# Three edits of order in a two-layer graph network: the first two groups, the seam between the passes, and the last group

## The chip, the cores and the metric

The kernel runs on one core of a Trainium2 chip. The metric is the device time of one execution in microseconds (us). The core has five engines, each with its own instruction queue that is worked off in order: PE (TensorE: matrix products; PEld is its weight load), DVE (VectorE), ACT (ScalarE), POOL (GpSimd) and SP (SyncE, here the issuer of nearly all DMAs). Every engine waits on semaphores for what the others produce. An instruction that waits holds up all that stand behind it on its engine.

## The reference

64 batches of 256 nodes with 512 features go through two layers. Everything is float32.

```python
# layer 0
h = relu(layernorm(x))                                    # per row of 512
x = x + einsum('bnd,do->bno', einsum('nm,bmd->bnd', adj, h), weight) + bias
# layer 1: 8 heads of 64
h = relu(layernorm(x))
q, k, v = h @ Wq + bq, h @ Wk + bk, h @ Wv + bv
scores = einsum('bqhd,bkhd->bhqk', q, k) / sqrt(64) + (1 - adj) * -1e9
x = x + einsum('bhqk,bkhd->bqhd', softmax(scores), v) @ Wo + bo
```

## The kernel before

**Groups and passes.** Two batches make a group, so there are NG = 32 groups, numbered 0 to 31. The first pass runs layer 0 over all groups and leaves two things in DRAM for each: the new x (`residual_g`) and its normalised, rectified and turned form (`hidden_g`). The second pass runs layer 1 over all groups. Between the two lies a seam: the last group of the first pass and the first group of the second.

**Products with seven instead of eight parts.** Every product of a weight with a group is cut into 2x2 blocks and done with seven block products (Strassen's scheme in Winograd's form). Its sums of operand blocks are prepared ahead. For activations they are named t1 to t4: t1 = b12 - b11, t2 = b22 - t1, t3 = b22 - b12, t4 = b21 - t2 (L442 to 446, class `Halves`). t2 needs t1, t4 needs t2, t3 needs neither. Written in capitals, T2 and T3 are the same two. For weights the sums are s1 to s4. In `project` (L456) the seven products follow one another on PE: a11·b11, a12·b21, s2·t2, s3·t3, s1·t1, a22·t4, s4·b22. The chain a11, s2·t2, s1·t1, s4 accumulates in one PSUM bank ("a"), and s3·t3, a22·t4 in another ("c"). Between two accumulations, another engine reads the bank out: where a product follows in the same bank, PE waits for this reading. In the second pass, from group 2 on, three of the seven are cut once more (`project2`, L541), and `block_sums_of` (L891) makes their inner sums (`both.sums` from the tokens, `last.sums` from t4) on POOL.

**Layer 0 of one group.** `moments` (L40) and `norm_scales` (L46, four small instructions on POOL named rs and nb) give the scales, `relu` in `ready` (L691) makes h on ACT. `feature_sums` (L745) and `last_feature_sum` make s1, s2, s3 and s4 of h on POOL, tile hs; s3 overwrites a part of h. `adjacency` (L759) multiplies h by the transposed adjacency matrix in seven products named py_ga, py_gb, py_gc; its own t1 to t4 of the adjacency matrix are made once by `adjacency_sums` (L734, tile adjT_t, four instructions on POOL). The result yT gets its t1 to t4 (tile t_y) on POOL. `layer0` (L810) multiplies by the weight (banks w_ga, w_gb, w_gc, of which a and c are filled with the bias by `seeded` on ACT, L255), adds x, takes the second moments, and leaves residual and hidden. Group 0 has a path of its own, `first_adjacency` (L710), with plain products py.

**Attention of one group and half.** `queries_keys` and `values` run seven products each for q, k and v. `score` (L964) multiplies q and k of one half of the heads (qd = 0 or 1), in four pieces numbered by c and b; DVE scales and masks (L980), POOL subtracts the row `top` (L986; in the last group piece c + b = 2 goes to DVE, L984), ACT takes exp (L991), POOL adds up two halves of keys (`key_sum`, L998, tile as). `attend` (L1000) multiplies by ones (pden, the denominators) and by v (pav), DVE inverts and multiplies (oT, L1027 and L1045), then the sums of oT (tile t_o) follow for the output product in `post`.

**What sets the order.** Nothing is scheduled automatically. The program is one list written out by hand with a clock: `tick()` advances it, `after(n, f)` puts f n ticks later, and what is due at one tick is put down in the order in which it was entered. The generators (`project`, `adjacency`, `layer0`) give control back after each product, and `run` ticks after each. So a number in `after` decides behind which instructions of its engine a piece of work stands; it sets no time. In pass 1 the loop at L1103 takes one product of `layer0(g)` and n products of `adjacency(g + 1)` per tick, with n from a list of seven. `ready`, `hidden_sums`, `score` and `attend` take such delays as arguments.

**The end.** `stats` collects sums that show an overflow; DVE reduces them to one number (L1165, L1166), PE multiplies it by ones (pf, L1168), DVE turns it into an integer (`flag`), and all engines read the flag to decide on a slower path that is not taken here.

Of the kernel before, what the change touches and what calls it, by code (L numbers as in the profile page):

```python
# [198 lines left out]
def kernel(  # L199
# [16 lines left out]
    nc = tc.nc  # L216
# [7 lines left out]
    NG = B // GB  # L224
# [42 lines left out]
    def after(delay, fn, *args):  # L267
        entered[0] += 1
        later.append((clock[0] + delay, entered[0], fn, args))
# [584 lines left out]
    H1T, HH, HO = {}, {}, {}  # L854
# [106 lines left out]

    A, AS = {}, {}

    def score(g, qd, sum_delay):  # L964


        pair = [act.tile([P, GB, 2 * NT, N], F32, tag="h", name=f"a_{g}_{qd}_{c}", bufs=2) for c in range(2)]
        for c in range(2):
            for b in range(GB):
                ps = [bank([P, NT * N], f"sc_{g}_{qd}_{c}{b}_{j}") for j in range(2)]  # L970
                q, k = Q[g][qd, b], K[g][qd, b]
                for kt in range(NT):
                    for j in range(2):
                        nc.tensor.matmul(ps[j][:, kt * N:(kt + 1) * N],  # L974
                                         k[j * HD:(j + 1) * HD, c, kt * P:(kt + 1) * P],
                                         q[j * HD:(j + 1) * HD, c, :], start=(kt == 0), stop=True,
                                         skip_group_check=True)
                a = A[c, b] = pair[c][:, b]
                for j in range(2):
                    nc.vector.scalar_tensor_tensor(a[:, j * NT:(j + 1) * NT, :].rearrange("p k n -> p (k n)"),  # L980
                                                   ps[j], SCALE, maskT_f, op0=ALU.mult, op1=ALU.add)
                    give(ps[j])
                if g == NG - 1 and c + b == 2:
                    after(2, lambda a: nc.vector.tensor_tensor(a, a, top_b, op=ALU.subtract), a)  # L984
                else:
                    nc.gpsimd.tensor_tensor(a, a, top_b, op=ALU.subtract)  # L986
                after((3, 4, 5, 8 if sum_delay > 3 else 6)[2 * c + b], exponent, a)
                after(sum_delay + 2 * c + b, key_sum, g, qd, c, b)

    def exponent(a):  # L990
# [9 lines left out]
    def attend(g, qd):  # L1000


        pd = bank([P, GN], f"pden_{g}_{qd}")
        po = [bank([P, GN], f"pav_{g}_{qd}_{f}") for f in range(2)]
        for b in range(GB):
            for h in range(4):
                nc.tensor.matmul(pd[h * 32:(h + 1) * 32, b * N:(b + 1) * N], ones[:, 0:32], AS[h // 2, b][:, h % 2, :],  # L1007
                                 start=(b == 0), stop=True, tile_position=(0, h * 32), skip_group_check=True)
        for b in range(GB):
            v = V[g][qd, b]  # L1010
            for k in range(NT):
                for f in range(2):
                    for h in range(4):
                        nc.tensor.matmul(po[f][h * 32:(h + 1) * 32, b * N:(b + 1) * N],  # L1014
                                         v[:, k, h * HD + f * 32:h * HD + f * 32 + 32],
                                         A[h // 2, b][:, (h % 2) * NT + k, :],
                                         start=(b + k == 0), stop=(k == NT - 1), tile_position=(0, h * 32),
                                         skip_group_check=True)
        i = g * HQ + qd
        if i == 0:  # L1020
            AS["rest"] = act.tile([P, 4, GN], F32, tag="yT1", name="rest")
        den, rden = AS["rest"][:, 0, :], AS["rest"][:, 1, :]
        nc.scalar.activation(den, pd, AF.Identity, accum_out=stats[:, 0, i:i + 1])  # L1023
        give(pd)

        def invert(c):
            nc.vector.reciprocal(rden[:, c * P:(c + 1) * P], den[:, c * P:(c + 1) * P])  # L1027

        early = 2 if g >= FIRST2 and (g, qd) != (NG - 1, 1) else 4
        for c in range(early):  # L1030
            invert(c)
        if qd == 0:

            last = g == NG - 1
            OT[g] = (xpool if last else act).tile([P, DC, GN], F32, tag="x" if last else "r", name=f"oT_{g}")
            HO[g] = Halves(f"o_{g}", [OT[g][:, :, k * N:(k + 1) * N] for k in range(GB)], 0 if last else 1)

        def note():
            nc.scalar.activation(den, rden, AF.Identity, accum_out=stats[:, 1, i:i + 1])

        def divide():
            for c in range(early, 4):
                invert(c)
            for f in range(2):
                nc.vector.tensor_tensor(OT[g][:, 2 * qd + f, :], po[f], rden, op=ALU.mult)  # L1045
                give(po[f])
            after(2 if (g, qd) == (NG - 1, 1) else 3, note)
            wait = 7 if (g, qd) == (NG - 2, 1) else 0
            sums = lambda: HO[g].sums(nc.gpsimd, ("t3", "t2", "t4") if qd else ("t1",))
            if wait:  # L1050
                after(wait, sums)
            else:
                sums()
            if qd and g >= FIRST2:
                block_outputs(g, nc.gpsimd, wait + 1 if g >= NG - 2 else 2)

        after(1, divide)

    def run(gen, steps=99):

        for _ in zip(range(steps), gen):
            tick()
# [12 lines left out]

    ready(0, (0, 0, 2, 2), (0, 2), (1, 1, 3, 3), batches=2)
    load(1)
    ready(1, (4, 4, 4, 4), (4,), (5, 5, 6, 6))
    after(6, feature_sums, 1)
    after(7, last_feature_sum, 1)  # L1080
    tick()
    turn_adjacency()
    adjacency_sums()
    split_bias(b0_r)
    tick()
    weight_sums(nc.vector, w0_sb, "0", (0, 0, 6, 7))
# [3 lines left out]
    steps = first_adjacency()  # L1090
# [3 lines left out]
    for g in range(NG - 1):  # L1094
        for fn, *args in side[g]:
            fn(*args)

        if g + 2 < NG:
            ready(g + 2, (1, 1, 1, 1), (1,), (3, 3, 3, 3))
            after(4, feature_sums, g + 2)  # L1100
            after(5, last_feature_sum, g + 2)
        weighted, turned = layer0(g, seeds), adjacency(g + 1)
        for i, n in enumerate((0, 0, 0, 1, 1, 2, 3) if g == 0 else (1, 1, 2, 2, 1, 0, 0)):  # L1103
            next(weighted)
            for _ in range(n):
                next(turned)
            if i == 5:
                seeds = seeded(b0_r, f"w_{g + 1}")
            tick()
            if i == 2 and g + 3 < NG:  # L1110
                load(g + 3)
        for rest in (weighted, turned):
            for _ in rest:
                pass
        if g == NG - 3:
            load_hidden(0)
    load_hidden(1)
    hidden_sums(0, 1, 1, 2, 2)
    steps = layer0(NG - 1, seeds)
    run(steps, 4)  # L1120
    run(queries_keys(0))
    score(0, 0, 6)
    tick()
    run(steps)
    hidden_sums(1, 1, 2, 6, 7)
    run(values(0))
    for g in range(NG):
        attend(g, 0)
        load_residual(g)
        if g + 2 < NG:  # L1130
            load_hidden(g + 2)
        score(g, 1, 5 if g < NG - 1 else 3)
        tick()
        if g == 0:
            for n, tag in ((4 * DC, "w0_sb"), (4, "w0_s1"), (4, "w0_s2"), (4, "w0_s4"), (4, "adjT"), (4, "b0_r")):
                t = const.tile([P, n, P], F32, tag=tag, name=f"spare_{tag}")
                spare.extend(t[:, i, :] for i in range(n))
        for n, at in (("q", 7),) if g == 0 else (("k", 1), ("v", 5)) if g == 1 else (("o", 2),) if g == 2 else ():
            for i, work in enumerate(block_sums(n)):
                after(at + i // 3, *work)  # L1140
        if g + 1 < NG:
            run(queries_keys(g + 1))
        else:
            last = post(g - 1, seed_outputs(g - 1))
            run(last, 6)
        attend(g, 1)
        if g + 1 < NG:
            score(g + 1, 0, 5)
            tick()
            steps = values(g + 1)  # L1150
            run(steps, 5)
            seeds = seed_outputs(g) if g + 2 < NG else None
            run(steps)
            if g + 2 < NG:
                hidden_sums(g + 2, 2, 3, 4, 5)
                if g + 2 >= FIRST2:
                    block_hidden(g + 2, 6)
                run(post(g, seeds))
# [5 lines left out]
    worst = small.tile([P, 1], F32, tag="worst", name="worst", bufs=1)  # L1164
    nc.vector.tensor_scalar(bad, stats.rearrange("p s i -> p (s i)"), BOUND, None, op0=ALU.is_gt)  # L1165
    nc.vector.tensor_reduce(worst, bad, AX.X, ALU.max)  # L1166
    pf = bank([1, 1], "pf")
    nc.tensor.matmul(pf, worst, ones[:, 0:1], start=True, stop=True)  # L1168
    nc.vector.tensor_copy(flag, pf)
# [36 lines left out]
```

## Time and profile before

| | us |
|---|---|
| three runs | 2666.66, 2666.79, 2671.13 |
| median | 2666.79 |
| the profiled execution | 2666.74 |
| its span (first to last instruction) | 2664.9 |

Busy time in that span: PE 2626.7 us (99%), POOL 1989.0 (75%), DVE 1865.7 (70%), ACT 971.8 (36%). PE is idle for 38.2 us in all: 9.4 before its first instruction, 7.0 after its last product, and the rest in gaps of 0.3 to 4.7 us in three places, the first 57 us, the seam (612 to 664 us) and the last 57 us. From 70 to 612 us, and from 670 to 2608 us, PE is busy in every slice.

In the timeline a row is: start, duration from the first to the last instruction of the row, engine, line, operation, tile written <- tiles read, shapes, count, and in brackets how long the engine was idle ahead of it and what ended that. A product of `project` is eight PE instructions of 256 columns and takes 1.73 us from start to start; a product of `adjacency` takes 0.89 us. The granted clock (PEclk) is 1.00 at full speed.

### The profile page before, as it was taken

What the parts mean: (1) busy time and instruction counts of PE and PEld (TensorE: products, weight loads), DVE (VectorE), ACT (ScalarE), POOL (GpSimd) and SP (SyncE); (2) the same over time, 40 slices, a digit from 0 to 9 for tenths busy, and PEclk for the clock granted to TensorE, in tenths of its full rate; (3) what the DMA queues carried; (4) which work ended last, traced back from release to release, by engine and by line L of the source; (5) the groups of instructions that cost most, each with busy time, mean ns of one, the idle gap of its engine ahead of it and who ended that gap; (6) DMA issues with size and microseconds to landing.
All of it is one profiled execution on the core that took longest, in us unless ns stands there. A gap on an engine that the chain in (4) does not pass through costs nothing. (4 is left out here: it accounts for less than half of the span.)

```text
span 2664.9 us, 51775 instructions
## 1 busy us (share of the span) xinstructions
PE 2626.7 (99%) x20076; PEld 2285.0 (86%) x20076; DVE 1865.7 (70%) x3860; ACT 971.8 (36%) x1875; POOL 1989.0 (75%) x1842
## 2 busy tenths in 40 slices
PE   7999999999999999999999999999999999999997
PEld 6999899998888888888888888888888888888885
DVE  5888788884467767667667666667677676667676
ACT  3444454543233333333333333333333333333332
POOL 5888887785778777777777777777777777777775
PEclk9999999999999999999999999999999999999999
DMA  5777666664122211111111111111222111111110
GB/s 123 202 189 187 172 167 181 168 165 98 46 64 55 58 48 48 49 48 49 49 48 48 49 48 48 49 48 49 65 65 62 50 48 48 49 48 49 49 48 34
DMA packets 281066, 211.04 MB, mean 79 GB/s; under 512 B 145904, under 2 KB 212976, under 8 KB 280816
## 3 DMA queue, kind: packets, MB, share of 16 engines
q1 hardware_dynamic: 280352, 207.15, 29.9%
q8 instruction: 161, 2.64, 0.4%
q14 instruction: 89, 0.73, 0.1%
q10 hardware_dynamic: 464, 0.52, 0.1%
HBM read 106.96 MB, written 100.66 MB: 78 GB/s over the span
## 5 line engine op out<-in xcount | busy, mean ns | idle before, releaser
L986 POOL TENSOR_TENSOR a<-a,top 128x1024 f32<-128x1024 f32 x254 | 592.4, 2367 | 486.9 <-DVE a L980 486.9
L980 DVE SCALAR_TENSOR_TENSOR a<-sc,maskT 128x512 f32<-128x512 f32 x512 | 311.9, 680 | 122.0 <-PE sc L974 122.0
L998 POOL TENSOR_TENSOR as<-a 128x512 f32<-128x512 f32 x256 | 318.9, 1279 | 4.2 <-ACT a L991 3.0
L991 ACT ACTIVATE a<-a 128x1024 f32<-128x1024 f32 x256 | 270.9, 1058 | 9.1 <-POOL a L986 7.8
L1027 DVE RECIPROCAL rest<-rest 128x128 f32<-128x128 f32 x256 | 224.3, 919 | 37.0 <-ACT rest L1023 37.0
L974 PE MATMUL sc<-q,k 64*128 64x256 f32 x2048 | 238.4, 382 | 0.0
L1014 PE MATMUL pav<-a,v 128*32 128x256 f32 x4096 | 234.0, 379 | 0.0
L974 PEld LDWEIGHTS sc<-q,k 64*128 64x128 f32 x2048 | 194.2, 187 | 44.7 <-issue 26.3
L1014 PEld LDWEIGHTS pav<-a,v 128*32 128x32 f32 x4096 | 133.5, 110 | 87.9
L1023 ACT ACTIVATE rest<-pden 128x512 f32<-128x512 f32 x64 | 38.2, 597 | 418.3 <-PE pden L1007 418.3
L665 DVE TENSOR_TENSOR k<-k,k 128x128 f32<-128x128 f32 (+1 forms) x300 | 96.0, 352 | 125.9 <-PE k L564 123.9
L42 DVE BATCH_NORM_STATS2 st<-x 128x6 f32<-128x512 f32 x256 | 173.1, 676 | 9.8 <-DMA x<-in_x_dram 7.6
L693 ACT ACTIVATE h<-x,nb,rs 128x512 f32<-128x512 f32 x128 | 94.0, 803 | 68.9 <-POOL nb L54 68.8
L665 DVE TENSOR_TENSOR x<-o,x 128x128 f32<-128x128 f32 (+1 forms) x360 | 111.1, 349 | 3.2
L820 ACT ACTIVATE h<-x,nb,rs 128x512 f32<-128x512 f32 x128 | 97.2, 807 | 43.9 <-POOL nb L54 40.7
L665 DVE TENSOR_TENSOR q<-q,q 128x128 f32<-128x128 f32 (+1 forms) x300 | 96.0, 352 | 13.7 <-PE q L564 11.7
L665 DVE TENSOR_TENSOR v<-v,v 128x128 f32<-128x128 f32 (+1 forms) x300 | 95.3, 351 | 14.4 <-PE v L564 11.3
L754 POOL TENSOR_TENSOR hs<-h 128x512 f32<-128x512 f32 x31 | 39.4, 1270 | 78.3 <-ACT h L693 56.5
L446 POOL TENSOR_TENSOR t_o<-oT 128x512 f32<-128x512 f32 x64 | 82.1, 1283 | 8.7 <-DVE oT L1045 8.7
L446 POOL TENSOR_TENSOR t_y<-yT 128x512 f32<-128x512 f32 (+1 forms) x65 | 81.9, 1260 | 7.3 <-ACT yT L804 5.9
L52 POOL TENSOR_TENSOR rs<-rs,mhalf 128x2 f32<-128x2 f32 (+1 forms) x97 | 80.1, 825 | 8.1
L446 POOL TENSOR_TENSOR t_h<-h1T,t_h 128x512 f32<-128x512 f32 x64 | 82.2, 1284 | 4.9
(4806 smaller groups left out, 6990.2 us busy)
## 6 DMA issues: line engine op xcount, KB each, us to landing
x<-in_x_dram SPq DMA_DIRECT2D x256, 128.0 KB, 3.0
residual<-x SPq DMA_DIRECT2D x256, 128.0 KB, 2.4
hidden<-r SPq DMA_DIRECT2D x128, 256.0 KB, 4.4
h1T<-hidden SPq DMA_DIRECT2D x64, 512.0 KB, 9.6
x<-residual SPq DMA_DIRECT2D x32, 1024.0 KB, 7.5
out_dram<-x SPq DMA_DIRECT2D x62, 512.0 KB, 4.2
w_sb<-in_L_gnn_weight_dram SPq DMA_DIRECT2D x1, 1024.0 KB, 6.9
wq_sb<-in_L_gnn_Wq_dram SPq DMA_DIRECT2D x1, 1024.0 KB, 6.4
```

The costliest lines, as they stand in the source:

```text
L42: nc.vector.bn_stats(st, src)
L446: eng.tensor_tensor(self.t[n][:, c, :], self.operand(p, c), self.operand(q, c), op=ALU.subtract)
L665: nc.vector.tensor_tensor(o, ps, u, op=ALU.add)
L693: nc.scalar.activation(H0[g][:, t, :], xt[:, t, :], AF.Relu, bias=nb[:, t % n:t % n + 1], scale=rs[:, t % n:t % n + 1])
L820: nc.scalar.activation(h1[:, k * NT + t, :], xt[:, k * NT + t, :], AF.Relu, bias=nb[:, t:t + 1], scale=rs[:, t:t + 1])
L974: nc.tensor.matmul(ps[j][:, kt * N:(kt + 1) * N], k[j * HD:(j + 1) * HD, c, kt * P:(kt + 1) * P], q[j * HD:(j + 1) * HD, c, :], start=(kt ...
L980: nc.vector.scalar_tensor_tensor(a[:, j * NT:(j + 1) * NT, :].rearrange("p k n -> p (k n)"), ps[j], SCALE, maskT_f, op0=ALU.mult, op1=ALU.add)
L986: nc.gpsimd.tensor_tensor(a, a, top_b, op=ALU.subtract)
L991: nc.scalar.activation(a, a, AF.Exp)
L998: nc.gpsimd.tensor_tensor(AS[c, b], a4[:, :, 0, :], a4[:, :, 1, :], op=ALU.add)
L1014: nc.tensor.matmul(po[f][h * 32:(h + 1) * 32, b * N:(b + 1) * N], v[:, k, h * HD + f * 32:h * HD + f * 32 + 32], A[h // 2, b][:, (h % 2) * ...
L1027: nc.vector.reciprocal(rden[:, c * P:(c + 1) * P], den[:, c * P:(c + 1) * P])
```

## The change

There are three parts.

1. **First two groups.** `adjacency_sums` moves from ahead of group 1's scales to behind them on POOL. The relus of group 1 move from between the copies of yT of group 0 to behind them on ACT. The sums of group 1's h (`feature_sums`) move from between the t_y of group 0 to behind them on POOL. The products of `adjacency(1)` are started one product earlier among those of `layer0(0)`: the list becomes 0, 0, 1, 2, 2, 2, 0. The sums of group 2's h come one tick later.
2. **Seam.** The last three products of `layer0(31)` stood behind the scores of group 0. They move between q and k of group 0. In the first `score`, piece c + b = 2 subtracts on DVE, exp and key sums come at fewer ticks, and the sums of group 1's hidden (t_h) move behind them.
3. **Last group.** The sums of oT: for group 30, t3 stays on POOL, t2 goes to DVE one tick later, t4 and the inner sums stay on POOL, one tick later. For group 31, t3 and t2 go to DVE. The product pf moves four products later, behind o_31a's s1·t1.

```diff
-    def score(g, qd, sum_delay):
+    def score(g, qd, sum_delay, exps=(3, 4, 5, 8)):
...
-                if g == NG - 1 and c + b == 2:
+                if (g == NG - 1 or (g, qd) == (0, 0)) and c + b == 2:
                     after(2, lambda a: nc.vector.tensor_tensor(a, a, top_b, op=ALU.subtract), a)
...
-                after((3, 4, 5, 8 if sum_delay > 3 else 6)[2 * c + b], exponent, a)
+                after(exps[2 * c + b], exponent, a)
...
-            wait = 7 if (g, qd) == (NG - 2, 1) else 0
-            sums = lambda: HO[g].sums(nc.gpsimd, ("t3", "t2", "t4") if qd else ("t1",))
-            if wait:
-                after(wait, sums)
+            wait = 0
+            if qd == 0:
+                HO[g].sums(nc.gpsimd, ("t1",))
+            elif g < NG - 2:
+                HO[g].sums(nc.gpsimd, ("t3", "t2", "t4"))
+            elif g == NG - 2:
+                wait = 8
+                after(7, HO[g].sums, nc.gpsimd, ("t3",))
+                after(8, HO[g].sums, nc.vector, ("t2",))
+                after(8, HO[g].sums, nc.gpsimd, ("t4",))
             else:
-                sums()
+                HO[g].sums(nc.vector, ("t3", "t2"))
+                HO[g].sums(nc.gpsimd, ("t4",))
...
-    ready(1, (4, 4, 4, 4), (4,), (5, 5, 6, 6))
-    after(6, feature_sums, 1)
-    after(7, last_feature_sum, 1)
+    ready(1, (4, 4, 4, 4), (4,), (8, 8, 8, 8))
+    after(4, adjacency_sums)
+    after(8, feature_sums, 1)
+    after(8, last_feature_sum, 1)
     tick()
     turn_adjacency()
-    adjacency_sums()
...
-            after(4, feature_sums, g + 2)
-            after(5, last_feature_sum, g + 2)
+            after(4 if g else 5, feature_sums, g + 2)
+            after(5 if g else 6, last_feature_sum, g + 2)
...
-        for i, n in enumerate((0, 0, 0, 1, 1, 2, 3) if g == 0 else (1, 1, 2, 2, 1, 0, 0)):
+        for i, n in enumerate((0, 0, 1, 2, 2, 2, 0) if g == 0 else (1, 1, 2, 2, 1, 0, 0)):
...
-    run(queries_keys(0))
-    score(0, 0, 6)
+    both = queries_keys(0)
+    run(both, 7)
+    run(steps)
+    run(both)
+    score(0, 0, 4, (3, 4, 5, 6))
     tick()
-    run(steps)
-    hidden_sums(1, 1, 2, 6, 7)
+    hidden_sums(1, 6, 6, 7, 7)
...
-        score(g, 1, 5 if g < NG - 1 else 3)
+        score(g, 1, *((5,) if g < NG - 1 else (3, (3, 4, 5, 6))))
...
     nc.vector.tensor_reduce(worst, bad, AX.X, ALU.max)
+    run(last, 3)
     pf = bank([1, 1], "pf")
```

## The prediction

> **What bounds the kernel now.** I read three views in this order: the busy shares, the waits of PE, and the timeline around each of those waits. The busy shares come first:
>
> ```profile
> PE 2626.7 (99%) x20076; PEld 2285.0 (86%) x20076; DVE 1865.7 (70%) x3860; ACT 971.8 (36%) x1875; POOL 1989.0 (75%) x1842
> ```
>
> PE is the bound. The change takes no product away, so it can only shorten the 38.2 us in which PE is idle, or the stretches in which PE runs at half clock. Of the idle time, 9.42 us lie ahead of the first matmul and 7.04 behind the last product; no edit touches the work there. What remains, some 21.7 us, is the ceiling in gaps. The waits of PE (us in total, times, longest) say which gaps there are:
>
> ```profile
> PE w_0a L453 <- ACT w_0a L255: 4.7, 1, 4.7
> ...
> PE pden L1007 <- POOL as L998: 3.2, 3, 1.6
> PE w_1a L453 <- POOL t_y L446: 2.6, 1, 2.6
> PE o_30a L453 <- DVE x L665: 2.3, 1, 2.3
> PE pf L1168 <- DVE worst L1166: 2.3, 1, 2.3
> PE o_31c L453 <- POOL t_o L446: 1.9, 1, 1.9
> ...
> PE v_0a L453 <- ACT v L924: 1.3, 1, 1.3
> ```
>
> Each happens once or a few times and lies in the first two groups, at the seam or in the last group. For the largest, the timeline of ACT (start, duration, work, and in brackets the idle time before):
>
> ```profile
> 21.53 1.52 ACT L693 ACTIVATE h<-x,nb,rs 128x512 f32<-128x512 f32 x2 [2.25 <-POOL nb L54]
> 22.95 0.56 ACT L727 COPY yT<-py 128x512 f32<-128x512 f32 x1
> 23.42 1.52 ACT L693 ACTIVATE h<-x,nb,rs 128x512 f32<-128x512 f32 x2
> 24.84 0.56 ACT L727 COPY yT<-py 128x512 f32<-128x512 f32 x1
> 25.31 0.58 ACT L255 COPY w_0a<-b_r 128x512 f32<-128x512 f32 x1
> ```
>
> ACT has nothing to do for 2.25 us because group 1's relus wait for nb, although the copies of yT behind them could run. The seed of w_0a thus comes at 25.9, while PE was free from 21.25. A gap costs a second time in the granted clock (from, to, busy times, PEclk, DMA share, GB/s):
>
> ```profile
> 57.00:57.40 0.40, 0.40 (x4) 1.00 0.93 338
> 57.40:60.80 3.40, 3.40 (x15) 0.50 0.90 239
> 60.80:61.20 0.40, 0.40 (x6) 0.98 0.39 77
> ```
>
> Three periods at half clock follow gaps (23.3 to 30.1, here, and 2624.23 to 2627.65). A row of eight products takes 2.60 us in this one where 1.89 is usual, and a whole period gives away about 1.7 us of work.
>
> **What the Trainium skill says.** "TensorE: Matmul & The Clock Gate", Part 1, has a free-running window of 3413 ns with half or full rate; the trace agrees, since its edges lie multiples of 3.413 us apart. In the same page, "Architectural detail", ACT and DVE are strict FIFO: the rows of ACT above show it. "SBUF — State Buffer", "Who interferes with whom", gives DVE and POOL a shared port pair with an exclusive lock; the trace shows it at group 31's subtraction on DVE, 2.30 us of which 1.23 are waiting for a POOL instruction, 1.07 work. "GPSIMD Engine Reference", 3.1, prices a two-input operation on POOL at 1.96 times DVE's; here 1.27 us against 0.55 to 0.69 for 512 columns.
>
> **First two groups: 6.7 us.** With the relus behind them, ACT's four yT copies and two seeds run at PE's pace: the seed of w_0a at 21.0, its end 21.6, yT complete at 22.6, relus 22.6 to 25.5. w_0a starts at 21.65 instead of 25.94, and its first two products take 1.73 each at full clock, where the cold window made them 3.58 together with gaps. That is a lead of over 4 us, part of which is handed back at once, because POOL is now late. Its order becomes: group 1's scales to 21.5; the adjacency sums, four of about 0.46, to 23.3; t1, t2 of yT (4 x 0.7, plus 0.5 for the lock) to 26.45; t3 and t4 to 28.9; s1, s2, s3 (1.25, 1.35, 1.2) to 32.7; s4 to 33.9; the scales of group 2 (1.95) to 35.85. On PE:
> - the product with t2 of yT waits 0.75 and ends at 27.8; then two products of group 1's py and one of w_0 to 30.5;
> - the py product of s3 waits for POOL until 32.75: a new gap of 2.2;
> - four products to 37.2, or to 38.9 if that gap makes the next window cold;
> - the py product of s1·t1 needs the copy at L789, which stands on ACT behind group 2's four relus (2.93), which wait for nb until 35.85: ready at 39.85, a new gap of 2.7, or 0.8 after a cold window. So the cold window of the first gap costs nothing by itself;
> - 6.13 of products bring w_1a to 45.98, before 48.11. Up to here the net gain is 2.1. POOL's sums for w_1a are in time (50.65 for 51.22), so the gap of 2.56 and its cold window, about 1.9, go as well.
>
> Sum: 2.1 + 2.6 + 1.9 = 6.6; the row positions give 6.7 (w_2a at 64.3 instead of 71.0). From there POOL is 2.2 us ahead of PE instead of 4.2; it works 15.4 of the 18.34 us per group, so it catches up. The x of group 4 lands at about 62, is used at 66. If the second gap brings a cold window, the gain is 5.0; if neither new gap arises, it is 6.7 + 2.2 + up to 2.7, near 11, but not more.
>
> **Seam: 1.7 us.** Before:
>
> ```profile
> 657.96 1.99 PE L453 MATMUL v_0a<-wv_s,t_h 128*128 128x256 f32 x8 [1.31 <-ACT v L924]
> ```
>
> and 0.72 more before pden and pav at 663 to 668, for key sums (as) on POOL. The three w_31 products moved between q and k push the scores, and what DVE, ACT and POOL do with them, behind; values follow the scores at once, so exps no longer stand before the copy of v_0a. One subtraction goes from POOL (2.37) to DVE (1.07 to 1.7), and the key sums two ticks earlier: as is ready at 662.15 for a pden at 662.4. The relus of h_31 stand ahead of the k copy, which makes the first k product wait about 0.4. 1.31 + 0.1 + 0.72 - 0.4 = 1.7. Ends: 0 if DVE's subtraction waits for a whole POOL instruction and as is 2 us late; 2.1 if k isn't late. h_1's sums come at 667, needed at 673.8.
>
> **Last group: 1.3 us out of two opposed parts.** The lines of before:
>
> ```profile
> 2619.90 1.75 DVE L1027 RECIPROCAL rest<-rest 128x128 f32<-128x128 f32 x2
> ...
> 2622.89 0.68 DVE L665 TENSOR_TENSOR x<-o_30a,x 128x512 f32<-128x512 f32 x1
> 2623.48 2.30 DVE L984 TENSOR_TENSOR a<-a,top 128x1024 f32<-128x1024 f32 x1
> ```
> ```profile
> 2616.47 7.00 POOL L986 TENSOR_TENSOR a<-a,top 128x1024 f32<-128x1024 f32 x3 [2.83 <-DVE a L980]
> ...
> 2627.14 1.27 POOL L446 TENSOR_TENSOR t_o<-oT 128x512 f32<-128x512 f32 x1
> ...
> 2630.12 4.95 POOL L998 TENSOR_TENSOR as<-a 128x512 f32<-128x512 f32 x4
> ```
>
> Group 30: t2 of oT goes to DVE ahead of these reciprocals. It reads two SBUF tiles, so it waits from 2619.9 for POOL's second subtraction, until 2621.13, and runs 0.57: 1.75 in all, by which the reciprocals, oT and x are later. Behind x stands PE: o_30a's next product starts at 2625.45 instead of 2623.71, gap 4 instead of 2.33. POOL's third subtraction is held 0.57, and t4 (1.27), formerly in an idle stretch, now comes after it: the four key sums, POOL's last work before pav, end at 2637.05 instead of 2635.07. PE's final gap there is set by POOL, so the loss is 1.97, not 1.75 + 1.97.
>
> Group 31: t3 and t2 of oT cost DVE 0.65 each instead of 1.3 on POOL. All rows being 1.97 later, t3 is there at 2646.2, t2 at 2646.85; o_31c starts at 2646.3 (before 2645.05, so 0.7 of its 1.92 gap are saved). pf now comes behind the last three products: PE no longer waits 2.29 for worst, and o_31a's last part starts at 2648.1 and, after 0.1 for POOL's sum, its last product at 2651.3 instead of 2652.62. The end is 1.3 earlier, which includes the loss of 1.97. pf then has to follow: the DVE chain to worst (x, 1.11, 0.28) ends near 2650.6, before the last product, so it costs nothing; without that cover it would add up to 0.4. The tail of 7.0 is unchanged. Ends: +2.5 (DVE's lock lost to two POOL subtractions, so group 30 loses 3.8 instead of 1.97, less 1.3 here) against a gain of 3.3 (no loss at group 30).
>
> **Sum.** 6.7 + 1.7 + 1.3 = 9.7. Span 2664.9 - 9.7 = 2655.2; profiled execution 2666.74 - 9.7 = 2657.0. The median of the runs is 0.05 above that execution: 2657.1, and I say 2657.2.
>
> **Rivals.**
> - *The clock takes part of it.* The second new gap instead of the first falls so that it makes a window cold, or the lock on t2 goes to POOL: 1.7 to 1.9 less, 2659. For: the phase of the window is free. Against: all edges of one execution lie on one grid, and the waiting DVE got the lock at the next instruction boundary in both cases shown.
> - *The start hands its lead back.* POOL's slack of 2.2 in the first pass is less than I work out, and group 2 or 3 stalls for the difference, or transfers are late: then only the seam and the end remain, 3.0, with the time at 2663.8, which isn't distinguishable from before. For: DMA share is 0.9 there. Against: the shift of relus is earlier, not later, from group 1 on.
> - *Slower: POOL becomes the bound of the first pass.* For later groups, the features' sums keep their tick, and POOL stays 2 us later behind PE. If each of 29 groups waited for it, 0.33 us would eat the 9.7; from 0.51 the kernel is over 0.2% slower, 2673 or more. For: POOL carries all these sums. Against: it has 2.9 us free in each group, and PE shows no wait in them now.
>
> **How the numbers follow.** A difference of 0.2% (5.3 us) is about what a measurement of this kernel tells from no change. Chances: forecast 0.60 (2655 to 2659.5), clock or lock 0.20 (2658 to 2661), lead handed back 0.10 (2661.5 to 2666), slower 0.04, and 0.06 for more gain (one of the two new gaps absent, 2650 to 2655). The bounds above put the range at 2653.5 to 2662.5, with about 0.1 outside on either side. Faster: 0.60 + 0.20 + 0.05 less a little at the edges = 0.82; same 0.14, slower 0.04.
>
> **What would show it.** Right: PE's w_0a starts near 21.7 with no wait for ACT's seed; new waits of py for POOL's hs and for ACT's L789 of about 2 us each; no wait of w_1a for t_y; w_2a near 64.3. No wait of v_0a for ACT; a k product waiting 0.4. DVE's t_o row at 2620 less the gain, with about 1.2 of waiting; key sums ending 2 later relative to the scores; no wait of pf; PE idle about 30 us. Wrong: waits of w_2a, w_3a and on for POOL; a half-clock period more than before; an o_31a wait for POOL's rest or t2o above 1 us.

## The result, and the profile after

The changed kernel takes 2659.73 us in the median of 12 runs (2658.45 to 2662.52), the kernel before 2666.61 beside it (12 runs, 2663.94 to 2671.13). The medians differ by 6.9. The ratio over all these runs is 0.9972, with a 95% interval of 0.9963 to 0.9981: some 7.5 us faster, 5.1 to 9.9 by the interval. The forecast was 9.7. The profiled execution took 2660.45, its span is 2658.7, 6.2 less than before. PE is idle for 34.7 of it (38.2 before, about 30 forecast), and its busy time is 2.7 shorter; the clock is at half for one period of 3.4 us during its work instead of four (the stretch from 23.3 to 30.1 before is two periods long).

The waits of PE in the changed kernel (engine and what it waited for, then us in total, times, longest):

```profile
...
PE o_30a L453 <- DVE x L665: 4.0, 1, 4.0
PE pden L1007 <- POOL as L998: 2.9, 3, 1.3
PE py_1a L770 <- ACT yT L789: 2.5, 1, 2.5
PE w_0a L453 <- POOL t_y L446: 2.3, 1, 2.3
PE py_1c L770 <- POOL h L754: 2.1, 1, 2.1
PE o_31c L453 <- DVE t_o L446: 1.4, 1, 1.4
...
PE w_0a L453 <- ACT w_0a L255: 0.3, 1, 0.3
...
PE k_0a L453 <- ACT k L907: 0.2, 1, 0.2
```

The waits that were to go are gone: ACT's seed (4.7 to 0.3), t_y of group 1 (2.6), v_0a (1.3), pf (2.3). The new ones stand where they were forecast: py for POOL's sums of h and for L789, o_30a at 4.0. The waits of pden are those of group 31 in both lists. The surprise in this list is the 2.3 of w_0a for t_y, where 0.75 was worked out.

To see where time went, I compare when PE starts the same product in both profiles. Negative is earlier than before:

| from | to | shift at the end of the stretch | share of the stretch | forecast |
|---|---|---|---|---|
| start | w_2b (73.63 to 68.98) | -4.65 | -4.65 | -6.7 |
| w_2b | w_31b, end of the first pass | -3.62 | +1.03 | 0 |
| w_31b | q_1b, behind the seam (674.00 to 668.51) | -5.49 | -1.87 | -1.7 |
| q_1b | group 31's last scores (2613.87 to 2609.04) | -4.83 | +0.66 | 0 |
| these scores | end of the span | -6.2 | -1.37 | -1.3 |

So seam and last group came as worked out. In this pair of executions the start gave 2.0 too little, and two stretches that no edit touches gave back 1.7.

The start, in the timeline of PE of the changed kernel (start, duration, work, idle time before it and what ended it):

```profile
21.64 1.99 PE L453 MATMUL w_0a<-w_sb,yT 128*128 128x256 f32 x8 [0.30 <-ACT w_0a L255]
...
27.68 2.25 PE L453 MATMUL w_0a<-w_s,t_y 128*128 128x256 f32 x8 [2.33 <-POOL t_y L446]
...
34.62 1.16 PE L770 MATMUL py_1c<-adjT_t,h 128*128 128x128 f32 x8 [2.07 <-POOL h L754]
...
41.78 1.16 PE L770 MATMUL py_1a<-adjT_t,hs 128*128 128x128 f32 x8 [2.50 <-ACT yT L789]
```

w_0a starts to 0.01 when it was said to, which is partly luck: PE's first matmul comes 0.57 later than before (9.99 and 9.42), and in five other profiles of this start w_0a lies between 20.74 and 21.67. What follows it is 1.6 to 2.0 later than worked out, because POOL's scales of group 1 begin at 21.07 instead of 19.20, and those wait for VectorE:

```profile
15.86 0.69 DVE L422 TENSOR_TENSOR w_s<-w_sb 128x512 f32<-128x512 f32 x1 [2.11 <-DMA w_sb<-in_L_gnn_weight_dram]
...
19.27 0.69 DVE L42 BATCH_NORM_STATS2 st<-x 128x6 f32<-128x512 f32 x1 [0.29 <-DMA x<-in_x_dram]
```

In the profile before, these two rows begin at 13.10 and 17.41. The weights took 9.8 us from issue to landing instead of 6.9, and group 1's x follows them in SP's queue. SP issues the same transfers in the same order at the start of both kernels. Whether the change caused it or chance did was the first question.

In the first pass, POOL and ACT of the changed kernel show this, once per group:

```profile
95.83 0.20 POOL L54 TENSOR_TENSOR nb<-nb,rs 128x4 f32<-128x4 f32 x1
99.07 1.27 POOL L754 TENSOR_TENSOR hs<-h 128x512 f32<-128x512 f32 x1 [3.04 <-ACT h L693]
...
117.64 1.27 POOL L754 TENSOR_TENSOR hs<-h 128x512 f32<-128x512 f32 x1 [1.81 <-ACT h L693]
```
```profile
96.06 2.93 ACT L693 ACTIVATE h<-x,nb,rs 128x512 f32<-128x512 f32 x4 [2.29 <-POOL nb L54]
```

POOL's idle time is no reserve: it makes nb, ACT makes the four relus of it in 2.93, and POOL, whose next instruction needs them, waits. The ring closes in 117.64 - 99.07 = 18.57 us, while PE needs 18.34. POOL falls back by 0.23 per group. The second wait is shorter (1.81) only because POOL spends 1.28 of it on a sum of weights that this group has besides; the period is the same. From the end of t3 on POOL to its first product on PE there were 2.07 us at group 1 before the change, and 0.07 at group 12; after it 1.17 at group 1 and 0.06 at group 6. From there on PE goes at the ring's pace, until extra work for PE at group 13 (about 3.5 us) gives POOL room again. My theory was then: chance at the start, the ring in the first pass, and the rest as forecast.

### The profile page after: what moved, and what is told of

Its sections match the earlier page's. It is cut to its first block, busy times and chain, and to the rows that moved or that the text cites. A ratio compares the mean times of both kernels' runs of the same rounds, so it can differ in the third digit from the quotient of the medians.

```text
span 2658.7 us, 51781 instructions
## 1 busy us (share of the span) xinstructions
PE 2624.0 (99%) x20076; PEld 2282.2 (86%) x20076; DVE 1869.5 (70%) x3864; ACT 970.5 (37%) x1875; POOL 1981.1 (75%) x1838
## 5 line engine op out<-in xcount | busy, mean ns | idle before, releaser
L1023 ACT ACTIVATE rest<-pden 128x512 f32<-128x512 f32 x64 | 38.2, 597 | 417.7 <-PE pden L1007 417.7
L446 POOL TENSOR_TENSOR t_o<-oT,t_o 128x512 f32<-128x512 f32 x62 | 79.2, 1277 | 12.3 <-DVE t_o L446 10.0
```

The costliest lines, as they stand in the source:

```text
L446: eng.tensor_tensor(self.t[n][:, c, :], self.operand(p, c), self.operand(q, c), op=ALU.subtract)
```

## The experiments

**Each part alone.** Three kernels, each the kernel before with one part of the change.

> Only the first two groups are changed. Theory: the start gains 4.7 at w_2a (up to 6.7 if group 1's x and weights land as early as before), and a ring of POOL and ACT in the first pass, 18.57 us per group against 18.34 of PE, takes some of it back until group 13, so that 3.2 to 3.6 are left: about 2663.2. Rival, the lead lasts: 4.7 or more are left, 2662 or less. Rival, the lead is handed back wholly: within 0.5 of before.

> Only the seam is changed. Theory: 1.7 to 1.9 less by itself, about 2664.8, with no wait of v_0a for ACT and none of pden for POOL. Rival: the seam's gain needs the lead of the first part, and is under 0.5 alone.

> Only the last group is changed. Theory: 1.3 to 1.4 less, about 2665.2, the sum of 1.7 to 2.0 lost at group 30 and 3.2 to 3.4 won at group 31. Rival: the loss at group 30 came of other rows standing differently, and is absent here: 3.3 less, 2663.3.

| | median | expected | ratio, 95% interval |
|---|---|---|---|
| only_start | 2665.71 | 2663.2 | 0.9990 (0.9981 to 0.9998) |
| only_seam | 2667.36 | 2664.8 | 0.9998 (0.9990 to 1.0006) |
| only_end | 2665.73 | 2665.2 | 0.9991 (0.9982 to 0.9999) |

The kernel before has a median of 2668.12 beside these, 1.5 more than beside the changed kernel, so the expected times are that much too low and the ratios count. Effects of 1 to 3 us hardly stand out of such intervals, so the profiles decide. In *only_start* the weights landed after 6.6 us, w_2b was 6.51 earlier (forecast 6.7), and the new waits had the sizes worked out:

```profile
PE py_1c L770 <- POOL h L754: 2.1, 1, 2.1
...
PE py_1a L770 <- ACT yT L789: 0.8, 1, 0.8
PE w_0a L453 <- POOL t_y L446: 0.4, 1, 0.4
```

From group 6 the lead shrank by about 0.24 per group, to 5.04 at w_13b, and was 5.47 at w_29b: the ring takes part of it back, but more is left than I wrote beforehand (3.2 to 3.6). By its number (4.7 or more left) the rival "the lead lasts" is met, since the start itself gained 6.5 and not 4.7; against it stands that the lead shrinks group by group. The rival that all is handed back is out. *only_seam* gained 1.88 between w_31b and q_1b (-1.73 to -3.61), with no wait of v_0a left: the seam needs no lead from the start. *only_end* has o_30a's wait of 4.03 again, so the loss at group 30 belongs to its edit. But from group 31's last scores to o_31a's last eight products, where the changed kernel takes 37.52 and before 38.75, it took 39.12: nothing gained. The granted clock shows why (from, to, busy times, PEclk, DMA share, GB/s):

```profile
2638.70:2641.50 2.80, 2.80 (x28) 1.29 (x32) 0.99 (x2) 1.28 (x3) 0.00 (x0) 0.50 0.02 6
```

A second half-clock period falls on pav, a row of 5.23 instead of 3.83. The same stretch took 40.41 in *only_start* and 40.53 in *only_seam*, whose last group is that of before, with a half-clock period behind pf's gap instead of inside o_30a (in *only_seam* it follows directly on another one). So the stretch has two lengths in either version: 38.75 or 40.41 to 40.53 without the edit, 37.52 or 39.12 to 39.17 with it. Like against like the edit is worth 1.2 to 1.4; which length comes moves the time by 1.6 to 1.8.

**The ring.** t4 of yT is not used until 6.1 us after t3 (93.45 and 99.58 in the changed kernel). Done behind the next scales, from group 2 on, it falls into the time in which POOL waits for relus:

```diff
-        after(3, YH[g].sums, nc.gpsimd, ("t3", "t4"))
+        after(3, YH[g].sums, nc.gpsimd, ("t3",))
+        after(5 if g > 1 else 3, YH[g].sums, nc.gpsimd, ("t4",))
```

> The changed kernel, but the sum t4 of yT is done two ticks later from group 2 on, behind the scales of the next group's h. Theory, ring: it falls in the time in which POOL waits for the relus, so POOL needs 17.3 us per group instead of 18.57, no longer falls back, and PE's waits for t_y from group 6 on (2.2 in all) are gone: about 2657.5. Rival: what is lost in the first pass is DMA or DVE (x of later groups): no change from the changed kernel, 2659.7, with the waits at the same groups.

2656.14 (ratio 0.9956, 0.9942 to 0.9970), 1.4 below what was expected; in its profile the weights landed early (6.1). Two groups of POOL's timeline:

```profile
91.41 0.20 POOL L54 TENSOR_TENSOR nb<-nb,rs 128x4 f32<-128x4 f32 x1
91.57 1.28 POOL L446 TENSOR_TENSOR t_y<-yT,t_y 128x512 f32<-128x512 f32 x1
94.66 1.27 POOL L754 TENSOR_TENSOR hs<-h 128x512 f32<-128x512 f32 x1 [1.82 <-ACT h L693]
...
112.94 1.27 POOL L754 TENSOR_TENSOR hs<-h 128x512 f32<-128x512 f32 x1 [0.57 <-ACT h L693]
```

The wait for the relus shrinks from 3.04 to 1.82, and from 1.81 to 0.57 in the group with the sum of weights. t3 is ready about 2.6 us ahead in most groups. PE takes 18.34 per group where the changed kernel took 18.5 to 18.6 (from w_6b to w_9b) and 18.4 to 18.6 (from w_28b to w_30b), and the lead does not shrink: -6.96 at w_2b, -7.05 at w_13b, -8.34 at w_31b. The ring is shown; transfers and VectorE, which are unchanged, are not the cause. The further growth is time that the kernel before also loses to the ring, from w_12b to w_14b and from w_27b to w_31b.

**The waits of the start.** One kernel puts group 2's relus behind the copies L786 and L789, one puts group 1's x ahead of the weights in SP's queue, and the first two sums of weights behind group 1's moments on VectorE.

```diff
-            ready(g + 2, (1, 1, 1, 1), (1,), (3, 3, 3, 3))
+            ready(g + 2, (1, 1, 1, 1), (1,), (3, 3, 3, 3) if g else (5, 5, 5, 5))
```

> The changed kernel, with group 2's relus on ACT behind the copies L786 and L789 instead of ahead of them. Theory: PE's wait for L789 (2.5, or 0.8 with a half-clock period before it) is gone, and w_1a starts earlier by up to as much; the relus themselves, which wait for nb, stand where they stood, so POOL's sums come no earlier than 2.3 at best, and of the lead about half may be lost at t_y of groups 1 and 2 or given back in the ring by group 13: 0.5 to 2.5 less at group 13. Rival: the wait only moves to hs of group 2 or t_y of group 1 on POOL, and w_2a starts no earlier.

```diff
+    load(1)
     w0_sb = load_weight(nc, const, w0, "w0_sb")
...
-    load(1)
...
-    weight_sums(nc.vector, w0_sb, "0", (0, 0, 6, 7))
+    weight_sums(nc.vector, w0_sb, "0", (2, 2, 6, 7))
```

> The changed kernel, with the transfer of group 1's x ahead of that of the weights on SP's queue, and the first two weight sums behind group 1's moments on VectorE. Theory: POOL's lateness in the first group stems from the arrival of group 1's x (scales of group 1 at 19 to 21 while POOL is idle from 15.5): they then stand near 15 to 16, the waits of w_0a for t_y (0.4 to 2.3) and of py_1c for s3 (2.1) go, w_0a itself starts as before if the weights land by 21, and w_2a is 3 to 5 earlier. Rival: the weights land after 21.6 and w_0a waits for them by more than is won; or POOL's own work sets the time, and the waits stay.

*relus_behind*: 2658.54 (0.9964, 0.9951 to 0.9978). Its weights landed late (9.1), its wait for t_y is 2.9, and that for L789 is gone; w_2b is 7.41 earlier than before, 2.8 more than in the changed kernel, and 5.31 at w_13b. *x1_first*: 2659.02 (0.9964, 0.9951 to 0.9978). Group 1's scales begin at 16.66 instead of 21.07, the wait for t_y is gone, that for s3 is 0.6 instead of 2.1, and w_2b 7.01 earlier; that is 2.4 more than in the changed kernel, where 3 to 5 were expected. The wait for L789 stays at 2.5. So the wait for L789 is due to the relus ahead of the copies, and that for t_y to the arrival of x. The wait for s3 is not due to x alone: it is 2.1 again in *best* below, which has the same order of transfers and starts w_0a 1.3 earlier. In both runs the ring then takes 2.1 and 1.8 until w_13b: what the start wins beyond POOL's pace is lost there.

**Chance or change at the start.** The changed kernel once more, unedited.

> The changed kernel again, unedited. Theory: what its profile lost against the forecast at the start (weights 9.8 from issue to landing, w_2a 4.65 earlier instead of 6.7) is chance of the transfers: with the weights landing in 6 to 7, w_2a is 6.5 earlier; with 9 or more, 3.7 to 4.7. The ring takes 1.1 to 1.6 of it until group 13 in either case. Rival: the change itself makes the weights late: 9 or more again and 4.7.

2659.97 (0.9972, 0.9961 to 0.9983). The weights took 9.0, and w_2b was 3.28 earlier, a little below the band written down; the ring took 1.7 of it until w_13b, a little above. Taken alone that would suit the rival. Over all profiles with the transfers in their old order it does not: with the old start, the weights took 6.9, 6.4, 8.8 and 9.4; with the new one 9.8, 9.0, 9.2, 9.1, 6.6 and 6.1. Late ones occur in both, early ones too. With late weights the old start loses as well (w_2b 1.5 later, in *only_end* and *pf_only*). Late against late, the new start is thus 4.8 to 6.2 ahead (*t2_pool*, *after_again* and the changed kernel against these two), and early against early 5.5 to 7.0 (*only_start* and *t4_later* against *only_seam* and the profile before). The 4.65 of the first comparison set a late execution against an early one. That lateness is frequent, and not tied to the change, is shown; that the change makes it no more frequent is not, with so few profiles.

**The last group.** One kernel puts the sums of group 30 back as they were (t2 on POOL, t4 and the inner sums one tick earlier), one moves only pf.

```diff
-                wait = 8
-                after(7, HO[g].sums, nc.gpsimd, ("t3",))
-                after(8, HO[g].sums, nc.vector, ("t2",))
-                after(8, HO[g].sums, nc.gpsimd, ("t4",))
+                wait = 7
+                after(7, HO[g].sums, nc.gpsimd, ("t3", "t2", "t4"))
```

> The changed kernel, with the sums of oT of group 30 as they were before (t3, t2 and t4 on POOL), those of group 31 still on VectorE. Theory: t2 on VectorE is what costs at group 30: o_30a's wait goes back from 4.03 to 2.33, the key sums are ready 1.8 to 2.0 earlier relative to the scores, and the end comes about 1.9 earlier relative to the scores, counted without half-clock periods, which move by up to 1.7 either way. Rival: the wait at pav is set by something else, and pav starts as late after the scores as in the changed kernel.

```diff
     nc.vector.tensor_reduce(worst, bad, AX.X, ALU.max)
+    run(last, 3)
     pf = bank([1, 1], "pf")
```

> The kernel before, with only pf moved behind three more products of the last group. Measured from group 31's last scores to the start of o_31a's last eight products (38.75 in the profile of before; 1.7 more where a half-clock period falls on them). Theory: pf's 2.29 wait was the larger part of what the last group wins; alone it gives 1.5 (o_31a then waits for POOL's t2 until 2647.6 and 0.3 for t2o), so 37.2, or 38.9 with a half-clock period. Rival: POOL's t2 and t2o, not pf, are what the end waits for, and pf alone gives under 0.5.

*t2_pool*: 2660.18 (0.9968, 0.9956 to 0.9981). Its weights landed late (9.2), w_2b was only 3.75 earlier, so the median tells nothing; the last group does. o_30a waits 2.33, and pav starts 21.26 after the scores instead of 23.10: 1.84 earlier. To o_31a's last eight it takes 35.69 instead of 37.52, 1.83 less. The lines of the changed kernel, POOL's subtractions and VectorE's t2:

```profile
2611.71 7.43 POOL L986 TENSOR_TENSOR a<-a,top 128x1024 f32<-128x1024 f32 x3 [5.49 <-DVE a L980]
2619.11 1.26 POOL L446 TENSOR_TENSOR t_o<-oT,t_o 128x512 f32<-128x512 f32 x1
```
```profile
2615.07 1.87 DVE L446 TENSOR_TENSOR t_o<-oT,t_o 128x512 f32<-128x512 f32 x1
2616.87 1.75 DVE L1027 RECIPROCAL rest<-rest 128x128 f32<-128x128 f32 x2
```

t2 takes 1.87 there for 0.69 of work (its length at group 31), and stretches POOL's three subtractions from 7.00 to 7.43. POOL's t4 (1.26), which needs t2, now stands behind them; in *t2_pool* it is done in POOL's idle time ahead of them. These two are 1.7 of the 1.84 by which the key sums begin later after the scores (18.09 and 16.25). *pf_only*: 2666.33 (0.9993, 0.9985 to 1.0001, not distinguishable), 36.91 in the same stretch instead of 38.75, 1.84 less against 1.5 expected. So pf's place alone is worth more than the whole part. The sums of group 31 on VectorE add to it: from pav to o_31a's last eight it is 14.43 in *t2_pool* and 15.64 in *pf_only*, with pav equally late after the scores in both (21.26, 21.27). Group 30's sums take 1.8 away. The three add up to the 1.2 of like against like.

**Together.** The four moves of the runs above (t4, relus, x, t2 back on POOL) in one kernel.

> The changed kernel with four further moves together: t4 of yT behind the next scales, group 30's t2 on POOL, group 2's relus behind the copies, group 1's x ahead of the weights. Theory: the gains lie in different places and add: 2.2 to 3.6 from t4, 3 to 5 from x, 0 to 2.5 from the relus (part of it the same as x's), 1.9 from t2: about 2651. Rival: the first pass hands back what the start wins, and it is no faster than with t4 and t2 alone, about 2655.

2650.50 (2649.31 to 2652.59), ratio 0.9933 (0.9920 to 0.9947): faster than both kernels, and what was expected (2651). Its waits of PE:

```profile
...
PE pden L1009 <- POOL as L1000: 3.2, 3, 1.6
PE o_30a L454 <- DVE x L666: 2.3, 1, 2.3
PE py_1c L771 <- POOL h L755: 2.1, 1, 2.1
PE o_31c L454 <- DVE t_o L447: 1.4, 1, 1.4
```

w_2b is 9.30 earlier than before, w_13b 9.39: all of the lead is kept. The seam gives 1.85 again, and the span is 14.1 shorter than before. What the start wins reaches the end once the ring no longer holds PE.

## Why the prediction was right or wrong

**The range and the sign were right**; 2659.73 lies in it, 2.5 above the forecast.

**First two groups, 6.7: right, with a term that depends on transfers.** Where x and the weights land early, *only_start* shows 6.51 and waits of 0.4, 2.1 and 0.8, against 0.75, 2.2 and 0.8 worked out. The step "group 1's scales to 21.5" took the landing of one execution for a constant: with 9.0 to 9.8 instead of 6.9 for the weights, they end 1.9 later in the changed kernel, and all behind them with it. The profile of before was itself an early one.

**"It catches up": wrong.** The step was "it works 15.4 of the 18.34 us per group, so it catches up". Busy time was taken for the time a group needs. The idle time stood inside a ring with ACT's relus, and the ring needs 18.57. It took back 1.5 of the lead from w_6b to w_13b; 1.03 are left of this at the end of the first pass, because the kernel before meets the ring too. The slower rival named this mechanism and rejected it by the same step ("it has 2.9 us free in each group"); it came, at 0.24 per group in a few groups instead of 29. The range holds all the same because the loss was small, which nothing in the working had shown: in this term it was luck. For t3, the sum at which POOL's lead runs out, that lead was 0.92 at group 2 in the changed kernel and 0.95 in *only_start*, not 2.2. The ring could be read from the rows of before, where t3's margin falls from 2.62 at group 2 to 0.07 at group 12.

**Seam, 1.7: right**, 1.85 to 1.88 in all eight profiles that have this edit, and nothing (0.05 at most) in the other three. The k product is idle for 0.16; from start to start it loses 0.33 (2.06 for 1.73), near the 0.4 of the sum.

**Last group, 1.3: right, term by term.** o_30a's gap was forecast at 4 and is 4.03, the loss at pav 1.97 and is 1.84; pf's wait is gone, and o_31c's gap is 1.39 where 1.2 was left. What was missing is that the half-clock period of before is not fixed to o_30a's gap. It can fall elsewhere or twice, so that in single executions the part shows from nothing to its full size.

**Second pass, 0: +0.66.** In the rows of the scores of group 4 and of group 19's second half PE takes about 0.34 longer than before. For group 4, the row of before and that of the changed kernel:

```profile
891.54 3.72 PE L974 MATMUL sc<-q,k 64*128 64x256 f32 x32
...
886.05 4.06 PE L974 MATMUL sc<-q,k 64*128 64x256 f32 x32
```

Both long rows stand in all six profiles of kernels that have the new start and t4 of yT in its old place, and in none of the other six. So they go with the program and not with a single execution; by what path stays open.

**Figures of the working.** Five are off, none of which enters the 9.7. The 3.58 for w_0a's first two products of before is the first alone (25.94 to 29.52); the two take 5.59. Between the products with t2 and s3 stands one product of py, not two; the 30.5 given there counts one. If neither new gap arose, 6.7 + 2.2 + 2.7 is 11.6, not near 11. And the bad end of the last group, 3.8 lost instead of 1.97, is +0.5 and not +2.5, as the 1.3 already contains the 1.97. The 0.55 for a two-input operation of 512 columns on VectorE stands in no row of before, where the shortest takes 0.65.

## What to carry to other kernels

The share of busy time of an engine that isn't the bound doesn't say whether it can catch up: follow what it waits for, and if that waits for the engine itself, the ring's period counts. Two rows of the same instruction in successive groups give it at once. Moving a sum that isn't urgent into the wait inside the ring is what made the lead won at the start last through the first pass. And where edits are worth one or two us each, compare starts of the same instruction, stage by stage, since the landing of the first transfers and the place of half-clock periods move single executions by as much.

## What was unexpected of the hardware

A 1 MB transfer with the same neighbours in its queue took 6.4 to 9.4 us to land with the old start and 6.1 to 9.8 with the new one, from one execution to the next. The same wait of 2.33 us at o_30a was followed by a half-clock period in three profiles (rows of 3.26, 3.17 and 2.58) and by none in three others (1.96 to 1.97), so the length of a gap alone doesn't decide it. The row of before and that of *t2_pool*:

```profile
2623.71 3.26 PE L453 MATMUL o_30a<-wo_s,t_o 128*128 128x256 f32 x8 [2.33 <-DVE x L665]
...
2620.40 1.97 PE L453 MATMUL o_30a<-wo_s,t_o 128*128 128x256 f32 x8 [2.33 <-DVE x L665]
```
